# Two half-size last blocks, and the per-group sums written ahead of exp: a graph layer on one core

## The chip, the cores and the metric

The kernel runs on one core of a Trainium2 chip. The metric is device time in microseconds (us) of one execution. Nine runs of the kernel before gave a median of 2788.3 us, from 2753.89 to 2828.07.

## The reference, cut to what matters

One message-passing layer of a graph network, with a residual and a layer norm, in float32: 12,500 nodes and 200,000 edges of 64 features, the edges sorted by their target `dst`.

```python
gates = ssp(edge_attr @ We1 + be1) @ We2 + be2              # ssp(v) = softplus(v) - log 2
gates = gates * (1 - sigmoid(5.0 * (edge_weight - 3.5)))    # the cutoff
h = ssp(concat(x[src], x[dst]) @ Wn1 + bn1) @ Wn2 + bn2
message_sum = zeros.at[dst].add(h * gates)
new = x + (ssp(message_sum @ Ws1 + bs1) @ Ws2 + bs2)
out = layernorm(x + new)                                    # over the 64 features, eps 1e-5
```

## The kernel before, in words

**Groups.** The edges are worked on in 391 groups of 512, each as four tiles of 128. The rows `x[src]` are gathered, 14 groups ahead, by GpSimd's indirect DMA (L230), and some by single-row DMAs that the queues of SP and ScalarE issue (L256). The targets of a half group lie within 42 nodes, so the part of layer 1 that belongs to `dst` comes from a table row range (L285), and the scatter is a matmul with a one-hot matrix (L292) that DVE makes.

**One step.** A Python loop writes the instructions down by hand; each engine works through its own instructions in that order, and waits on semaphores of the others where data asks for it. With `i` as the step, TensorE does: transposes of group i+1 (L306, L303), the biases of layer 1 (L318, group i+1) and of layer 2 (L353, group i), `scatter(i-1)` (L382), `layer1_edge(i+1)` (L323), `layer1_node(i+1)` (L329) and `layer2(i)` (L360, L365). ScalarE does `xcopy` (L313, PSUM to SBUF, what L329 reads), `exps` (L340) and `logs` (L343) of group i+1, and issues nine row DMAs between them. DVE does `window(i-1)` (L399: two additions of the scattered sums, 64 x 42 each, into the SBUF tile `sums`), `hcut(i)` (L374), `message(i)` (L378, what the next scatter reads), `softplus(i+1)` (L348, what layer 2 of group i+1 reads) and `onehot(i+3)` (L292). The place in `sums` at which `window` adds is read from SBUF into registers of DVE's sequencer (L390).

**Buffers.** `z` is a PSUM tile of two banks, of which two exist. Layer 1 of group g writes three quarters of the tile: L323 a half of the first bank, L329 the other half and the first half of the second bank. `exps(g)` reads all three. The last quarter is lent: `scatter(g-2)` writes its sums into the free quarter of `zs[g]`, and `window(g-2)` reads them there. The framework orders the accesses to such a tile by the order in which the program writes them down, whatever the part of the tile: in this kernel `window(i-1)` is written behind `exps(i+1)`, and so the first addition waits for ScalarE's exp of group i+1 (the built program has that one wait on it). `exps(i+1)` itself waits for L329 and for an older softplus.

**Blocks.** The nodes are finished in blocks of 512 (a first one of 212, then 24 of 512): as soon as all edges of a block must have been added, `node_block` makes eleven parts of it (fetch of x, first layer L418, clamp, exp and log, centring, second layer L446 and L449, addition, square, variance, root, scaling, store), and `BLOCK_STEPS` spreads these over later steps. The last block waits for the last group and runs alone behind it.

Of the kernel before, what the change touches and what calls it, by code (L numbers as in the profile page):

```python
# [57 lines left out]
P = 128  # L58
# [12 lines left out]
BEHIND = 4  # L71


BLOCK_STEPS = ((2, 3, 4, 4, 6, 7, 8, 9, 10, 14), (2, 3, 3, 4, 5, 6, 7, 8, 9, 10), (1, 2, 1, 2, 3))
ROWS = (7, 9)
READ = 8
ROWS_FROM = -1
# [8 lines left out]
def node_blocks(N):  # L86

    first = N % NB
    assert N > NB and first % 2 == 0 and first <= HE
    sizes = ([first] if first else []) + [NB] * (N // NB)  # L90
    return [(sum(sizes[:i]), n) for i, n in enumerate(sizes)]


# [29 lines left out]
def gnn_resnorm_kernel(ctx: ExitStack, tc: tile.TileContext, a: dict, out: bass.AP, E: int):  # L123
# [277 lines left out]
    def node_block(first, n, pool):  # L401


        nq = -(-n // HE)
        p = min(P, n // 2)
        t = {}
        rows = slice(first, first + n)

        def tile3(name):
            return pool.tile([P, 2, 2, D], F32, name=name, bufs=3)[:p, :nq]  # L410

        def small(name):
            return pool.tile([P, 2, 2], F32, name=name, bufs=2)[:p, :nq]

        def hidden(z):
            t["z"] = z[:, :HE]
            for q in range(nq):
                nc.tensor.matmul(t["z"], ws1[:, q].rearrange("f o d -> f (o d)"),  # L418
                                 sums[:, first + q * HE : first + (q + 1) * HE], start=q == 0, stop=q == nq - 1,
                                 skip_group_check=True)  # L420

        def fetch():
            t["y"] = tile3("y")
            nc.sync.dma_start(t["y"], x[rows, :].rearrange("(q p k) d -> p q k d", q=nq, k=2))

        def center():
            mean = small("mean")
            nc.vector.tensor_reduce(mean, t["y"], AX.X, OP.add)
            nc.vector.scalar_tensor_tensor(t["y"], mean.to_broadcast([p, nq, 2, D]), -1.0 / D, t["y"], OP.mult, OP.add)

        def clamp():
            t["l"], t["zb"] = (pool.tile([P, HE], F32, name=name, bufs=2) for name in ("l_s", "zb"))
            nc.vector.tensor_scalar(t["l"], t["z"], packed["bs1"], BIG, OP.add, OP.min)
            nc.vector.tensor_scalar(t["zb"], t["z"], packed["bs1"], None, OP.add)

        def logs():
            nc.scalar.activation(t["l"], t["l"], AF.Exp)
            nc.scalar.activation(t["l"], t["l"], AF.Ln, bias=half, scale=0.5)

        def ssp():  # L440
            nc.vector.scalar_tensor_tensor(t["l"], t["zb"], -LN2, t["l"], OP.add, OP.max)

        def layer2(z):
            slots = t["l"].rearrange("f (p k) -> f k p", k=2)
            t["u"] = z[:p, :HE].rearrange("p (q k d) -> p q k d", q=2, k=2)
            nc.tensor.matmul(z[:p, :HE], ones3[:, :p], rs3.rearrange("q k d -> q (k d)"), start=True,  # L446
                             stop=False, skip_group_check=True)
            for k in range(2):
                nc.tensor.matmul(t["u"][:, :, k, :], slots[:, k, :p], ws2, start=False, stop=k == 1,  # L449
                                 skip_group_check=True)  # L450
# [12 lines left out]
        def root():  # L463
            t["r"] = small("rstd")
            nc.scalar.activation(t["r"], t["v"], AF.Ln, bias=eps[:p], scale=1.0 / D)
            nc.scalar.activation(t["r"], t["r"], AF.Exp, scale=-0.5)

        def scale():

            v, r = small("scaled"), t["r"]  # L470
            nc.vector.tensor_scalar(v, t["v"], 1.0 / D, EPS, OP.mult, OP.add)
            nc.vector.tensor_mul(v, v, r)
            nc.vector.scalar_tensor_tensor(v, v, -0.5, r, OP.mult, OP.mult)
            nc.vector.scalar_tensor_tensor(r, v, 1.5, r, OP.add, OP.mult)
            nc.vector.tensor_mul(t["y"], t["y"], r.to_broadcast([p, nq, 2, D]))

        def store():
            nc.sync.dma_start(out[rows, :].rearrange("(q p k) d -> p q k d", q=nq, k=2), t["y"])
# [10 lines left out]
    with tc.manual_schedule():  # L489
# [124 lines left out]
        with tc.tile_pool(name="finish", bufs=1) as finish:  # L614
# [12 lines left out]
            for i in range(-1, last - 1):  # L627
                now = parts.pop(i, [])
                early = [part for part in now if part.tensor]
                at(load, i + LOADS)  # L630
                read_rows(i, 0, ROWS[0])
                fetch(i, 0, ROWS[0])
                if i >= 0:
                    at(gather, i + AHEAD)
                transposes(i + 1, ("load", i + 1), ("gather", i + 1), ("onehot", i + 1))
                xcopy(i + 1)
                read_rows(i, 1, ROWS[1])
                fetch(i, 1, ROWS[1] - 6)
                layer1_bias(i + 1)
                at(layer2_bias, i)  # L640
                if i >= 1:
                    scatter(i - 1, zs[i + 1][:, 1, HE : HE + 2 * W])
                layer1_edge(i + 1)
                layer1_node(i + 1)
                exps(i + 1)
                fetch(i, 1, 3)
                logs(i + 1)
                fetch(i, 1, 3)
                at(window, i - 1)
                at(layer2, i)  # L650
                for part in early:
                    part.tensor(tx_tile())
                at(hcut, i)
                at(message, i)
                softplus(i + 1)
                for part in early:
                    part.others()
                at(onehot, i + 3)
                for part in now:
                    if not part.tensor:  # L660
                        part.others()
                complete = i
                if blocks and complete >= blocks[0][1] - PREPARE and not begun:
                    begun = node_block(*blocks[0][0], finish)
                    begun.pop(0).others()
                if blocks and complete >= blocks[0][1]:
# [6 lines left out]
            assert len(blocks) == 1 and begun and not parts  # L673


            begun.pop(2).others()
            transposes(last, ("load", last), ("gather", last), ("onehot", last))
            xcopy(last)
            layer1_bias(last)
            layer2_bias(last - 1)  # L680
            scatter(last - 2, zs[last][:, 1, HE : HE + 2 * W])
            layer1_edge(last)
            layer1_node(last)
            for some in (edge, node):
                exps(last, some)
                logs(last, some)
            square, variance, root, scale, store = (part.others for part in rest)
            square()
# [6 lines left out]
            layer2_edge(last)  # L695
            softplus(last, node)
# [4 lines left out]
            variance()  # L701
            root()
# [5 lines left out]
            hidden, clamp = begun.pop(0)  # L708
            hidden(gh_tile())
            scale()  # L710
            clamp()
            store()
            for part in begun:
                node_part(part)


# [150 lines left out]
```

## Time and profile before

| | |
|---|---|
| median of nine runs | 2788.3 us |
| the profiled execution | 2772.95 us, its span 2771.2 us |
| TensorE busy | 2201.4 us (79%), granted clock 0.824 of full |
| DVE, ScalarE, GpSimd busy | 1050.1, 968.3, 1431.7 us |
| from the last scatter's first matmul (2756.20 us) to the end | 15.0 us |
| `window`, both additions (L399) | 0.41 us |

The profile is one execution recorded by the hardware. A row of the timeline has start, duration, engine, line, operation, tiles and shapes, the number of instructions, and in brackets the idle time of the engine before it with what ended it. PE is TensorE, PEld its weight loads, ACT ScalarE, POOL GpSimd. A float32 matmul shows as two records. Ends of matmuls are modelled, so what waits for a matmul can start later than its row ends. The granted clock is recorded in pieces that are multiples of 3.41 us, at 1.0 or 0.5.

### The profile page before, as it was taken

How to read it: one execution, taken by the hardware profiler on the slowest of the kernel's cores; microseconds unless marked ns; L12 is line 12 of the kernel's file. 1: busy time of each engine (PE TensorE's matmuls, PEld its weight loads, DVE VectorE, ACT ScalarE, POOL GpSimd, SP SyncE). 2: the span in 40 equal slices, each digit the busy share in tenths (PEclk: the TensorE clock that was granted, in tenths of full speed). 3: DMA queues.
4: the chain of work that ended last, by engine and by line, in shares of the span. 5: the costliest groups of instructions: out<-in, count | busy, mean ns of one | idle time of the engine just before them, and what ended most of it. 6: DMA issues, size and time to landing. Idle time of an engine off the chain costs nothing.

```text
span 2771.2 us, 47838 instructions
## 1 busy us (share of the span) xinstructions
PE 2201.4 (79%) x11373; PEld 1765.4 (64%) x11373; DVE 1050.1 (38%) x2767; ACT 968.3 (35%) x1318; POOL 1431.7 (52%) x1520
## 2 busy tenths in 40 slices
PE   2478877788888887888877887888878788888788
PEld 1456666666666666666666666666666667666676
DVE  1333333333334333333333333434333433344345
ACT  0133333333333333333333333333333333333344
POOL 7245555545555555555555555555555545555530
PEclk9997788877888788778888879888888877777888
DMA  6222222212222222212222222222222222222220
GB/s 155 94 54 49 46 46 48 46 44 46 48 46 47 49 50 48 47 45 50 51 46 49 52 47 52 51 51 52 49 49 47 51 47 49 51 50 49 49 51 24
DMA packets 150911, 143.53 MB, mean 52 GB/s; under 512 B 51887, under 2 KB 98395, under 8 KB 150626
## 3 DMA queue, kind: packets, MB, share of 16 engines
q1 hardware_dynamic: 94090, 88.26, 11.3%
q0 software_dynamic: 48512, 49.77, 9.8%
q10 hardware_dynamic: 8024, 2.37, 0.4%
q8 instruction: 97, 1.59, 0.2%
q14 instruction: 188, 1.54, 0.2%
HBM read 130.59 MB, written 9.63 MB: 51 GB/s over the span
## 4 chain that ended last, share of the span: by engine, by line
PE 62%; issue 13%; another core or an unknown queue 9%; DVE 8%; ACT 4%; ACTq 3%; DVEq 1%; DMA 0%; SPq 0%
PE z L329 15%; PE gh L365 11%; PE z L382 11%; PE tx L306 7%; PE gh L360 7%; PE z L323 6%; ACT xT L313 3%; ACTq L256 3%; DVE h L374 3%; DVE msg L378 2%; PE gh L353 1%; PE z L318 1%; PE tx L418 1%; DVE sums L399 1%
## 5 line engine op out<-in xcount | busy, mean ns | idle before, releaser
L230 POOL DMA_INDIRECT xg<-in_x,src_i x1516 | 1431.5, 944 | 1246.1 <-PE z L382 418.7
L329 PE MATMUL z<-xT,wns 106*128 106x256 f32 x1564 | 572.5, 503 | 113.2 <-ACT xT L313 101.1
L340 ACT ACTIVATE u<-z 128x768 f32<-128x768 f32 x392 | 317.0, 809 | 920.4 <-issue 473.3
L382 PE MATMUL z<-xg,msg 128*128 128x84 f32 x1556 | 310.7, 330 | 347.1 <-DVE msg L378 247.8
L399 DVE TENSOR_TENSOR sums<-sums,z 64x42 f32 x778 | 152.9, 197 | 1121.1 <-issue 913.2
L382 PEld LDWEIGHTS z<-xg,msg 128*128 128x128 f32 x1556 | 243.1, 223 | 506.5 <-DVE msg L378 328.0
L329 PEld LDWEIGHTS z<-xT,wns 106*128 106x128 f32 x1564 | 374.6, 249 | 250.5 <-ACT xT L313 164.8
L365 PE MATMUL gh<-consts,s 128*128 128x64 f32 x3128 | 474.6, 305 | 0.0
L365 PEld LDWEIGHTS gh<-consts,s 128*128 128x128 f32 x3128 | 474.1, 231 | 0.0
L313 ACT COPY xT<-tx 106x512 f32<-106x512 f32 x391 | 228.5, 584 | 671.4 <-PE tx L306 248.6
L343 ACT ACTIVATE u<-u,one 128x768 f32<-128x768 f32 x392 | 365.9, 934 | 68.9 <-issue 56.8
L348 DVE SCALAR_TENSOR_TENSOR s<-u,z 128x768 f32<-128x768 f32 x392 | 369.0, 942 | 11.2 <-ACT u L343 10.1
L360 PEld LDWEIGHTS gh<-consts,s 128*128 128x128 f32 x1564 | 320.9, 253 | 45.4 <-DVE s L348 2.0
L374 DVE TENSOR_TENSOR h<-gh,cut 128x256 f32<-128x256 f32 x391 | 165.9, 424 | 449.5 <-PE tx L306 157.7
L323 PE MATMUL z<-eT,consts 128*128 128x256 f32 x782 | 312.0, 488 | 0.0
L360 PE MATMUL gh<-consts,s 128*128 128x128 f32 x1564 | 310.3, 334 | 1.7 <-DVE s L348 1.7
L306 PE MATMUL tx<-consts,xg 128*106 128x128 f32 x1517 | 260.1, 296 | 6.5 <-DMA wns<-table 6.5
L306 PEld LDWEIGHTS tx<-consts,xg 128*106 128x106 f32 x1517 | 202.1, 160 | 10.7 <-issue 8.0
L378 DVE TENSOR_TENSOR msg<-gh,h 128x256 f32<-128x256 f32 x391 | 165.8, 424 | 13.4
L353 PE MATMUL gh<-row,ones 3*128 3x512 bf16 x391 | 158.1, 404 | 0.0
L323 PEld LDWEIGHTS z<-eT,consts 128*128 128x128 f32 x782 | 147.9, 235 | 0.7 <-issue 0.7
L292 DVE TENSOR_TENSOR xg<-consts,rel 128x168 f32<-128x168 f32 x391 | 127.6, 327 | 0.0
(93 smaller groups left out, 604.0 us busy)
## 6 DMA issues: line engine op xcount, KB each, us to landing
xr<-in_x ACTq DMA_DIRECT2D x3328, 0.2 KB
eT<-in_eT SPq DMA_DIRECT2D x195, 256.0 KB
xr<-in_x SPq DMA_DIRECT2D x2688, 0.2 KB
xg<-in_x,src_i POOLq DMA_INDIRECT x1516
wns<-table SPq DMA_DIRECT2D x782, 21.0 KB
table<-tb SPq DMA_DIRECT2D x14, 448.0 KB
sums<-in_xT SPq DMA_DIRECT2D x7, 455.0 KB
y<-in_x SPq DMA_DIRECT2D x24, 128.0 KB
```

The lines of the kernel that those rows point to most:

```text
L230: note(("gather", g), nc.gpsimd.indirect_dma_start(out=xg[:, k, :D], out_offset=None, in_=x, in_offset=bass.IndirectOffsetOnAxis(ap=src_i[ ...
L306: ins = nc.tensor.transpose(tx[:, k, :], xgs[g][:, k, :DW], ident)
L313: note(("xcopy", g), nc.scalar.copy(xT, xTs[g]))
L323: nc.tensor.matmul(zs[g][:, 0, :HE], we1.rearrange("a h d -> a (h d)"), eTs[g], start=False, stop=True, skip_group_check=True)
L329: nc.tensor.matmul(zn, wns[:, g % REST, h, :], xTs[g][:, h], start=True, stop=True, skip_group_check=True)
L340: nc.scalar.activation(us[g][:, part], z_of(g)[:, part], AF.Exp)
L343: nc.scalar.activation(us[g][:, part], us[g][:, part], AF.Ln, bias=one)
L348: nc.vector.scalar_tensor_tensor(ss[g].rearrange("p i t e -> p (i t e)")[:, part], us[g][:, part], BIG, z_of(g)[:, part], OP.min, OP.max)
L360: nc.tensor.matmul(v[:, 0, t], ss[g][:, 0, t, :], we2, start=False, stop=False, skip_group_check=True)
L365: nc.tensor.matmul(ghs[g][:, 1, 2 * t + h, :], ss[g][:, 1 + h, t, :], wn2, start=False, stop=h == 1 and t == 1, skip_group_check=True)
L374: nc.vector.tensor_mul(hs[g], ghs[g][:, 1], cut[:, g, :].to_broadcast([P, K, D]))
L382: ins = nc.tensor.matmul(sc, msgs[g][:, 2 * t : 2 * t + 2, :].rearrange("p h f -> p (h f)"), xgs[g][:, 2 * t : 2 * t + 2, D:DW], start=t = ...
```

## The change

Three edits:

1. In the loop, `window(i-1)` is written behind `scatter(i-1)`, ahead of layer 1 and `exps` of group i+1; before, it stood behind `logs(i+1)` and its row DMAs. The same is done for the last groups, behind the loop.
2. The last 512 nodes are two blocks of 256. In such a block a tile has one node of 64 features for each of two halves in a partition (`kk = 1`) where others have two, so each instruction works on half as many columns.
3. The first of these two blocks is begun beside the last two groups; only the second waits for the last group. The block ahead of them keeps one more part (its square) in the steps.

```diff
-BLOCK_STEPS = (..., (1, 2, 1, 2, 3))
+BLOCK_STEPS = (..., (1, 2, 1, 2, 3, 4))
...
-    sizes = ([first] if first else []) + [NB] * (N // NB)
+    sizes = ([first] if first else []) + [NB] * (N // NB - 1) + [HE] * 2
...
+        kk, cols = 2, HE
+        if n == HE:
+            nq, kk, cols = 2, 1, P
...
-            return pool.tile([P, 2, 2, D], F32, name=name, bufs=3)[:p, :nq]
+            return pool.tile([P, 2, kk, D], F32, name=f"{name}{kk}", bufs=3 if kk == 2 else 2)[:p, :nq]
...
-            t["z"] = z[:, :HE]
+            t["z"] = z[:, :cols]
...
                 if i >= 1:
                     scatter(i - 1, zs[i + 1][:, 1, HE : HE + 2 * W])
+                at(window, i - 1)
                 layer1_edge(i + 1)
                 layer1_node(i + 1)
                 exps(i + 1)
                 fetch(i, 1, 3)
                 logs(i + 1)
                 fetch(i, 1, 3)
-                at(window, i - 1)
                 at(layer2, i)
...
+                if i == last - 2 * PREPARE:
+                    first_half, final = (node_block(*block, finish) for block, _ in blocks[-2:])
...
             scatter(last - 2, zs[last][:, 1, HE : HE + 2 * W])
+            window(last - 2)
+            scale()
+            store()
             layer1_edge(last)
             layer1_node(last)
...
-            window(last - 2)
+            z = z_tile()
+            hidden, clamp = first_half.pop(0)
+            hidden(z[:, 0, :])
+            clamp()
...
+            logs1.others()
+            scatter(last - 1, tx_tile()[:, : 2 * W])
             softplus(last, node)
             layer2_node(last)
-            hcut(last - 1)
-            message(last - 1)
-            scatter(last - 1, tx_tile()[:, : 2 * W])
...
+            window(last - 1)
+            ssp1.others()
+            hidden2(z[:, 1, :])
             hcut(last)
             message(last)
+            add1()
             scatter(last, tx_tile()[:, : 2 * W])
-            window(last - 1)
+            square1.others()
             window(last)
...
```

More of the change, by code (lines that the diff above doesn't have):

```diff
@@ L71 @@
 BEHIND = 4
-BLOCK_STEPS = ((2, 3, 4, 4, 6, 7, 8, 9, 10, 14), (2, 3, 3, 4, 5, 6, 7, 8, 9, 10), (1, 2, 1, 2, 3))
+BLOCK_STEPS = ((2, 3, 4, 4, 6, 7, 8, 9, 10, 14), (2, 3, 3, 4, 5, 6, 7, 8, 9, 10), (1, 2, 1, 2, 3, 4))
 ROWS = (7, 9)
@@ L409, in tile3 @@
         def tile3(name):
-            return pool.tile([P, 2, 2, D], F32, name=name, bufs=3)[:p, :nq]
+            return pool.tile([P, 2, kk, D], F32, name=f"{name}{kk}", bufs=3 if kk == 2 else 2)[:p, :nq]
         def small(name):
-            return pool.tile([P, 2, 2], F32, name=name, bufs=2)[:p, :nq]
+            return pool.tile([P, 2, kk], F32, name=f"{name}{kk}", bufs=2)[:p, :nq]
         def hidden(z):
-            t["z"] = z[:, :HE]
+            t["z"] = z[:, :cols]
             for q in range(nq):
                 nc.tensor.matmul(t["z"], ws1[:, q].rearrange("f o d -> f (o d)"),
-                                 sums[:, first + q * HE : first + (q + 1) * HE], start=q == 0, stop=q == nq - 1,
+                                 sums[:, first + q * cols : first + (q + 1) * cols], start=q == 0, stop=q == nq - 1,
                                  skip_group_check=True)
@@ L423, in fetch @@
             t["y"] = tile3("y")
-            nc.sync.dma_start(t["y"], x[rows, :].rearrange("(q p k) d -> p q k d", q=nq, k=2))
+            nc.sync.dma_start(t["y"], x[rows, :].rearrange("(q p k) d -> p q k d", q=nq, k=kk))
         def center():
@@ L428, in center @@
             nc.vector.tensor_reduce(mean, t["y"], AX.X, OP.add)
-            nc.vector.scalar_tensor_tensor(t["y"], mean.to_broadcast([p, nq, 2, D]), -1.0 / D, t["y"], OP.mult, OP.add)
+            nc.vector.scalar_tensor_tensor(t["y"], mean.to_broadcast([p, nq, kk, D]), -1.0 / D, t["y"], OP.mult, OP.add)
         def clamp():
-            t["l"], t["zb"] = (pool.tile([P, HE], F32, name=name, bufs=2) for name in ("l_s", "zb"))
+            t["l"], t["zb"] = (pool.tile([P, cols], F32, name=f"{name}{kk}", bufs=2) for name in ("l_s", "zb"))
             nc.vector.tensor_scalar(t["l"], t["z"], packed["bs1"], BIG, OP.add, OP.min)
@@ L443, in layer2 @@
         def layer2(z):
-            slots = t["l"].rearrange("f (p k) -> f k p", k=2)
-            t["u"] = z[:p, :HE].rearrange("p (q k d) -> p q k d", q=2, k=2)
-            nc.tensor.matmul(z[:p, :HE], ones3[:, :p], rs3.rearrange("q k d -> q (k d)"), start=True,
+            slots = t["l"].rearrange("f (p k) -> f k p", k=kk)
+            wide = 2 * kk * D
+            t["u"] = z[:p, :wide].rearrange("p (q k d) -> p q k d", q=2, k=kk)
+            nc.tensor.matmul(z[:p, :wide], ones3[:, :p], rs3.rearrange("q k d -> q (k d)")[:, :wide], start=True,
                              stop=False, skip_group_check=True)
-            for k in range(2):
-                nc.tensor.matmul(t["u"][:, :, k, :], slots[:, k, :p], ws2, start=False, stop=k == 1,
+            for k in range(kk):
+                nc.tensor.matmul(t["u"][:, :, k, :], slots[:, k, :p], ws2, start=False, stop=k == kk - 1,
                                  skip_group_check=True)
@@ L474, in scale @@
             nc.vector.scalar_tensor_tensor(r, v, 1.5, r, OP.add, OP.mult)
-            nc.vector.tensor_mul(t["y"], t["y"], r.to_broadcast([p, nq, 2, D]))
+            nc.vector.tensor_mul(t["y"], t["y"], r.to_broadcast([p, nq, kk, D]))
         def store():
-            nc.sync.dma_start(out[rows, :].rearrange("(q p k) d -> p q k d", q=nq, k=2), t["y"])
+            nc.sync.dma_start(out[rows, :].rearrange("(q p k) d -> p q k d", q=nq, k=kk), t["y"])
         return [Part(None, fetch), Part(hidden, clamp), Part(None, logs), Part(None, center), Part(None, ssp),
@@ L661, in gnn_resnorm_kernel @@
                         part.others()
+                if i == last - 2 * PREPARE:
+                    first_half, final = (node_block(*block, finish) for block, _ in blocks[-2:])
+                    first_half.pop(0).others()
+                    final.pop(0).others()
+                if i == last - PREPARE:
+                    first_half.pop(2).others()
+                    final.pop(2).others()
                 complete = i
-                if blocks and complete >= blocks[0][1] - PREPARE and not begun:
+                if len(blocks) > 2 and complete >= blocks[0][1] - PREPARE and not begun:
                     begun = node_block(*blocks[0][0], finish)
                     begun.pop(0).others()
-                if blocks and complete >= blocks[0][1]:
+                if len(blocks) > 2 and complete >= blocks[0][1]:
                     steps = next(steps for steps in BLOCK_STEPS if i + steps[-1] < last - 1)
@@ L672, in gnn_resnorm_kernel @@
                     begun = None
-            assert len(blocks) == 1 and begun and not parts
-            begun.pop(2).others()
+            assert len(blocks) == 2 and blocks[0][1] < last and not begun and not parts
+            variance, root, scale, store = (part.others for part in rest)
+            variance()
             transposes(last, ("load", last), ("gather", last), ("onehot", last))
             xcopy(last)
+            root()
             layer1_bias(last)
@@ L686, in gnn_resnorm_kernel @@
                 logs(last, some)
-            square, variance, root, scale, store = (part.others for part in rest)
-            square()
-            window(last - 2)
+            z = z_tile()
+            hidden, clamp = first_half.pop(0)
+            hidden(z[:, 0, :])
+            clamp()
             for g in range(last - 1, last + 1):
@@ L695, in gnn_resnorm_kernel @@
             layer2_edge(last)
+            hcut(last - 1)
+            message(last - 1)
+            logs1, ssp1, (hidden2, add1), square1, variance1, root1, scale1, store1 = first_half
+            logs1.others()
+            scatter(last - 1, tx_tile()[:, : 2 * W])
             softplus(last, node)
             layer2_node(last)
-            hcut(last - 1)
-            message(last - 1)
-            scatter(last - 1, tx_tile()[:, : 2 * W])
-            variance()
-            root()
+            window(last - 1)
+            ssp1.others()
+            hidden2(z[:, 1, :])
             hcut(last)
             message(last)
+            add1()
             scatter(last, tx_tile()[:, : 2 * W])
-            window(last - 1)
+            square1.others()
             window(last)
-            hidden, clamp = begun.pop(0)
+            hidden, clamp = final.pop(0)
             hidden(gh_tile())
-            scale()
+            variance1.others()
             clamp()
-            store()
-            for part in begun:
+            root1.others()
+            final.pop(0).others()
+            scale1.others()
+            store1.others()
+            for part in final:
                 node_part(part)
```

## The prediction

> **What bounds the kernel now.** I read the page first (busy shares, clock row, chain), then the timeline of one step near the end, where nothing disturbs the loop, then the groups behind L399, and last the step by step times of the whole loop.
>
> ```profile
> PE 2201.4 (79%) x11373; PEld 1765.4 (64%) x11373; DVE 1050.1 (38%) x2767; ACT 968.3 (35%) x1318; POOL 1431.7 (52%) x1520
> PEclk9997788877888788778888879888888877777888
> PE 62%; issue 13%; another core or an unknown queue 9%; DVE 8%; ACT 4%; ACTq 3%; DVEq 1%; DMA 0%; SPq 0%
> ```
>
> No engine is full; TensorE carries 62% of the chain (1718 of 2771 us), and its granted clock is under full from the third slice on. The loop is a ring, seen in the timeline of steps 383 and 384:
>
> ```profile
> 2723.49 0.42 DVE L378 TENSOR_TENSOR msg<-gh,h 128x256 f32<-128x256 f32 x1
> 2723.83 0.94 DVE L348 SCALAR_TENSOR_TENSOR s<-u,z 128x768 f32<-128x768 f32 x1
> 2723.97 0.68 PE L382 MATMUL z<-xg,msg 128*128 128x84 f32 x4
> ...
> 2724.48 0.63 PE L323 MATMUL z<-eT,consts 128*128 128x256 f32 x2
> 2724.69 0.33 DVE L292 TENSOR_TENSOR xg<-consts,rel 128x168 f32<-128x168 f32 x1
> ...
> 2724.95 1.03 PE L329 MATMUL z<-xT,wns 106*128 106x256 f32 x4
> ...
> 2726.02 0.81 ACT L340 ACTIVATE u<-z 128x768 f32<-128x768 f32 x1 [1.97 <-PE z L329]
> ...
> 2726.86 0.41 DVE L399 TENSOR_TENSOR sums<-sums,z 64x42 f32 x2 [1.51 <-ACT u L340]
> ...
> 2727.31 0.42 DVE L374 TENSOR_TENSOR h<-gh,cut 128x256 f32<-128x256 f32 x1
> ```
>
> The message (L378) ends at 2723.91; TensorE scatters it (2723.97), goes on without a pause to L323 (2724.48), L329 and layer 2, then DVE takes h (2727.31) and the next message, 4.27 us a step. TensorE pauses only while DVE does h and message (0.50 us before L382). DVE's softplus and one-hot run beside L382 and L323, and the additions (L399) wait for exp:
>
> ```profile
> L399 DVE TENSOR_TENSOR sums<-sums,z x778: 190/198/205, 153.5 to 2750.9; 64x42 f32 x195
> ...
>   issue: 913.2, 313
>   ACT u L340: 202.9, 79
> ```
>
> Over steps 20 to 369 a step takes 6.79 us, not 4.27: 0.98 from message to the scatter's end, 4.92 from there to h, 0.88 for h and message.
>
> **The change in the loop.** DVE's order does not change: additions, h, message, softplus, one-hot. What changes is who waits for whom. Written behind the scatter, the additions wait for L382 alone, no longer for exp. But they now stand ahead of L323, L329 and exp in the program, all of which use the z tile whose last quarter the additions read. In the built program of the changed kernel L323 waits for the second addition, and exp does; before, L323 waited for nothing of DVE. So the ring gets a new link: scatter, additions, L323. And the additions stand in DVE's queue behind softplus (0.94) and one-hot (0.33) of the step before, and behind whatever block part lies there. Behind the waiting L323, on TensorE, stand L329 and layer 2, and h, message and the next scatter wait for those.
>
> *Price of the new wait, one clean step.* From the rows above: one-hot ends at 2724.69 + 0.33 = 2725.02; additions 2725.05 to 2725.46; L323 some 0.07 later (one semaphore, as from L378's end to L382), at 2725.53, not 2724.48. That is 1.05 us of TensorE standing still; the step becomes 5.32 us.
>
> *Over the loop.* For steps 10 to 384 I took from the trace, for each step, the last of three things: scatter's semaphore, end of the DVE instruction ahead of the additions, end of their register load (L390, 0.53 us) plus 0.1; added 0.03 + 0.41 + 0.07, and compared the sum with the start of L323. L323 comes 1.37 us later in the mean (quarter points 0.94, 1.05, 1.85); in 150 steps the scatter is last, in 157 DVE, in 68 the register load. Part of that costs nothing, since L329 in many steps waited for the copied xT anyway: L329 comes 1.05 us later in the mean (quarter points 0.73, 1.01, 1.26). 389 steps x 1.05 = **+408 us**. Exp's own new wait adds nothing: it follows L329, which now comes later than the additions.
>
> *What goes.* In 56 of 365 steps h started within 0.07 us of the additions' end, on average 0.40 us after layer 2's modelled end: at most 56 x 0.40 = **-22 us**.
>
> *What may swallow some.* In 222 steps layer 2's semaphore came later than its modelled end, by 312 us in total; what delays it I can't name. If it is a point in time, the new wait vanishes in it; if it is a duration, nothing does. Bounds 0 and -312. I take a quarter, **-78 us**, nearer to none, because steps with a block's first layer (L418, 1.1 us of TensorE) were 0.9 us longer than the mean.
>
> *The clock.* Between 200 and 2650 us the trace has 441 pieces of 3.41 us at full clock and 276 at half. 146 of the full ones are followed by half. In those TensorE's rows cover 48% in the mean (22 to 65% for nine in ten), and the longest pause is 1.6 us at the median; in the 295 others 86%, and 0.39. So the clock falls after a piece with some 1.4 us or more of pauses. The new pause of 1.05 us stands 0.68 us from the old one of 0.50: a piece that holds both has 1.55 us of pauses, 55% covered. I take it that half, not a third, of the full pieces are then followed by half; with the rise as now (146 of 276) the share at half goes from 38 to 49%, the mean clock from 0.81 to 0.76. TensorE's 1718 us of the chain x (0.81/0.76 - 1) = **+113 us**. Bounds: 0 if no more pieces fall; if all steps run at half clock, a step is some 7.5 us (the slow steps of the trace: 1.2 + 5.4 + 0.88) plus 0.75 for the wait, 8.25, so (8.25 - 6.79) x 389 = +568 in place of all the terms here.
>
> The Trainium skill ("TensorE: Matmul & The Clock Gate", section "HAM oscillation — how this bites in real kernels") warns only of idle gaps over about 3.4 us. By that rule a pause of 1.05 us costs no clock, and the sum would be 113 us lower; this trace's clock fell after much shorter pauses, so the row decides.
>
> **The change at the end.** From 2756.2 us on, a block of 512 runs alone; half the columns save: L418 2.05 to about 1.0, L449 1.22 to 0.6, three ScalarE steps by 0.11 each (exp of 256 columns takes 0.38, of 768 0.81), five DVE steps by 0.13 each (0.42 at 256, 0.94 at 768): 2.6 us. The first half's work beside the last two groups puts two small matmul pairs (about 1.4 us at full clock) on TensorE between 2748 and 2757 and some 2 us on DVE, which is in the ring; if all of it is exposed +3.4, if none 0; I take 2. Net **-1 us**. Its scaling and store, and the fetches of both halves, lie beside other steps and are among what DVE's queue holds. This whole edit cannot be measured here.
>
> **Sum.** 2773 + 408 - 22 - 78 + 113 - 1 = 3193 us for a profiled execution like this one, which stood 15 us below the median of the nine: **3205 us**.
>
> **Rivals.**
> 1. *The late semaphores swallow the wait.* For: they come in three steps of five, and often exceed 1 us. Against: only 193 steps have over 0.3 us, and in the last 90 us, which have next to none, the wait is bare. 2773 + 408 - 22 - 312 = 2847 without a lower clock, 2960 with it: 2920 in the middle, with the 15 us.
> 2. *The clock stays at half.* For: even the undisturbed steps get 1.55 us of pauses, and a slow clock makes the ring longer. Against: at half clock TensorE's work fills the pieces again, and 146 of 276 slow pieces were followed by full ones. 2773 + 568 + 15: about 3360, up to 3500 if the late semaphores come on top.
> 3. *Not slower: h freed of the additions wins.* Place: the start of h, where 56 steps waited for the additions. Price: -22 us, and -3 at the end: 2763. It decides if the new wait is under 0.06 us a step, that is if DVE is free 0.4 us before the scatter ends. The one-hot ends before the scatter by that much in about one step of twenty; in the clean step it ends 0.37 us after it.
> 4. *Nothing happens in the loop*, because DVE's order is the same, and L323's wait is met before it counts: 2790. The clean step speaks against it as against the third.
>
> **Chances.** Forecast 0.64 (3040 to 3330), first rival 0.14, second 0.18, third 0.02, fourth 0.02. The range of 2930 to 3420 leaves out the last two, a third of the first and a third of the second. A change of under 1% could not be told from none here: faster by over 1% 0.01, within 1% 0.03, slower by over 1% 0.96.
>
> **What would show it.** In the profile after: L323 idles with the additions (L399) as releaser, some 300 to 500 us in total; the additions wait for L382 and no longer for L340; in the last 80 us, where the gathers are over, the step is 5.3 us or more instead of 4.27; the mean clock is about 0.76. The forecast is wrong if L323's idle time is there but the time from scatter to h is not longer (first rival), if the clock row reads 5 and 6 throughout (second), or if the additions end before the scatter's successor could start (third).

## The result and the profile after

The changed kernel took 3182.62 us (median of 20 runs, 3156.9 to 3204.74), the kernel before 2786.42 us (62 runs). The ratio is **1.1441 [1.1413, 1.1469]**: slower, and within 23 us of the 3205 us predicted. Medians count every run; the ratios, here and below, leave out the executions that stood clearly above the others of their kernel. Its profiled execution took 3193.88 us, with a span of 3192.0 us and a granted clock of 0.742 in place of 0.824.

From the page of the changed kernel: busy time of each engine, the clock row, the chain.

```profile
PE 2501.6 (78%) x11378; PEld 2011.7 (63%) x11378; DVE 1032.2 (32%) x2779; ACT 968.5 (30%) x1323; POOL 1432.1 (45%) x1520
PEclk9967677677677776778777676777776676777777
PE 61%; DVE 17%; issue 9%; another core or an unknown queue 7%; DVEq 4%; DMA 1%; POOL 1%; ACT 0%; ACTq 0%; SPq 0%; POOLq 0%
```

TensorE has five matmuls more than before, and 300 us more of busy time (2501.6 against 2201.4): the same work at a lower clock. The row that read 7 and 8 reads 6 and 7. DVE, 8% of the chain before, is 17% now.

The timeline of two steps near the end of the changed kernel (start, duration, engine, line, operation, tiles):

```profile
3130.59 0.42 DVE L378 TENSOR_TENSOR msg<-gh,h 128x256 f32<-128x256 f32 x1
3130.94 0.94 DVE L348 SCALAR_TENSOR_TENSOR s<-u,z 128x768 f32<-128x768 f32 x1
3131.07 0.68 PE L382 MATMUL z<-xg,msg 128*128 128x84 f32 x4
3131.80 0.33 DVE L292 TENSOR_TENSOR xg<-consts,rel 128x168 f32<-128x168 f32 x1
3132.04 0.41 DVE L465 TENSOR_REDUCE var<-y 128x4 f32<-128x256 f32 x1
3132.37 0.40 DVE L399 TENSOR_TENSOR sums<-sums,z 64x42 f32 x2
3132.82 0.70 PE L323 MATMUL z<-eT,consts 128*128 128x256 f32 x2 [1.07 <-DVE sums L399]
...
3138.48 0.41 DVE L399 TENSOR_TENSOR sums<-sums,z 64x42 f32 x2 [0.56 <-issue]
3138.94 1.22 PE L323 MATMUL z<-eT,consts 128*128 128x256 f32 x2 [1.62 <-DVE sums L399]
```

The new link is there as it was read from the program: softplus, one-hot, here also a block's reduction (L465), then the additions, and 0.05 us after those L323, with TensorE idle for 1.07 us. One step later the pause is 1.62 us and L323 takes 1.22 us in place of 0.70: the clock has gone to half. The 0.56 us ahead of the additions of that step are in part the load of their place in `sums` by DVE's sequencer (DVEq), 0.35 us on the chain of this execution:

```profile
3137.92 0.35 DVEq L390
```

All instances of the additions in the changed kernel: what ended their own wait, and who waited for them.

```profile
L399 DVE TENSOR_TENSOR sums<-sums,z x778: 130/197/205, 151.5 to 3171.3; 64x42 f32 x195
...
  PE z L382: 45.0, 71
  issue: 29.1, 65
...
  ACT u L340: 813.0, 196
  PEld z L323: 393.9, 359
  PE z L323: 331.6, 359
```

They wait for the scatter (L382) and never for exp (L340). Instead L323 waits for them in 359 recorded cases: 331.6 us of idle TensorE. All instances of L323 in the kernel before, which idled 0.7 us in all:

```profile
L323 PE MATMUL z<-eT,consts x782: 379/417/795, 141.1 to 2748.0; 128*128 128x256 f32 x196
...
  issue: 0.7, 2
```

For steps 20 to 369 I took the mean time of each part of a step from the rows of both traces, in us:

| | before | after | |
|---|---|---|---|
| step, from one h to the next | 6.79 | 7.83 | +1.04 |
| end of scatter to start of L323 | −0.18 | 0.99 | +1.17 |
| end of L323 to start of L329 (wait for xT) | 0.19 | −0.19 | −0.38 |
| L323, L329 and layer 2 themselves | 4.14 | 4.77 | +0.63 |
| modelled end of layer 2 to h | 0.95 | 0.57 | −0.38 |

### The profile page after: what moved, and what is told of

It reads as the page before. It is cut to its first block, busy times and chain, and to the rows that moved or that the text cites. A ratio compares the mean times of both kernels' runs of the same rounds, so it can differ in the third digit from the quotient of the medians.

```text
span 3192.0 us, 47723 instructions
## 1 busy us (share of the span) xinstructions
PE 2501.6 (78%) x11378; PEld 2011.7 (63%) x11378; DVE 1032.2 (32%) x2779; ACT 968.5 (30%) x1323; POOL 1432.1 (45%) x1520
## 4 chain that ended last, share of the span: by engine, by line
PE 61%; DVE 17%; issue 9%; another core or an unknown queue 7%; DVEq 4%; DMA 1%; POOL 1%; ACT 0%; ACTq 0%; SPq 0%; POOLq 0%
PE z L329 16%; PE gh L365 13%; PE z L323 11%; PE gh L360 8%; DVE h L374 4%; PE tx L306 4%; PE z L382 4%; DVE sums L399 4%; DVE s L348 3%; DVEq L390 3%; DVE xg L292 2%; DVE msg L378 1%; PE gh L353 1%; PE z L594 1%
## 5 line engine op out<-in xcount | busy, mean ns | idle before, releaser
L230 POOL DMA_INDIRECT xg<-in_x,src_i x1516 | 1431.9, 945 | 1630.9 <-PE z L382 522.6
L340 ACT ACTIVATE u<-z 128x768 f32<-128x768 f32 x392 | 317.0, 809 | 1587.8 <-issue 903.0
L323 PE MATMUL z<-eT,consts 128*128 128x256 f32 x782 | 395.7, 601 | 383.4 <-DVE sums L399 331.6
L329 PE MATMUL z<-xT,wns 106*128 106x256 f32 x1564 | 639.2, 553 | 1.0 <-ACT xT L313 1.0
L365 PEld LDWEIGHTS gh<-consts,s 128*128 128x128 f32 x3128 | 539.8, 259 | 0.1
L365 PE MATMUL gh<-consts,s 128*128 128x64 f32 x3128 | 531.9, 330 | 0.0
L329 PEld LDWEIGHTS z<-xT,wns 106*128 106x128 f32 x1564 | 449.3, 287 | 107.4 <-ACT xT L313 1.4
L382 PEld LDWEIGHTS z<-xg,msg 128*128 128x128 f32 x1556 | 241.0, 222 | 360.6 <-DVE msg L378 315.7
L382 PE MATMUL z<-xg,msg 128*128 128x84 f32 x1556 | 307.9, 328 | 200.9 <-DVE msg L378 173.6
L323 PEld LDWEIGHTS z<-eT,consts 128*128 128x128 f32 x782 | 160.5, 256 | 451.0 <-DVE sums L399 393.9
L360 PEld LDWEIGHTS gh<-consts,s 128*128 128x128 f32 x1564 | 371.1, 291 | 55.6 <-DVE s L348 0.7
L360 PE MATMUL gh<-consts,s 128*128 128x128 f32 x1564 | 359.2, 375 | 0.4 <-DVE s L348 0.4
L306 PE MATMUL tx<-consts,xg 128*106 128x128 f32 x1517 | 282.4, 314 | 6.5 <-DMA wns<-table 6.5
L306 PEld LDWEIGHTS tx<-consts,xg 128*106 128x106 f32 x1517 | 220.3, 172 | 10.7 <-issue 8.0
```

The costliest lines, as they stand in the source:

```text
L230: note(("gather", g), nc.gpsimd.indirect_dma_start(out=xg[:, k, :D], out_offset=None, in_=x, in_offset=bass.IndirectOffsetOnAxis(ap=src_i[ ...
L306: ins = nc.tensor.transpose(tx[:, k, :], xgs[g][:, k, :DW], ident)
L323: nc.tensor.matmul(zs[g][:, 0, :HE], we1.rearrange("a h d -> a (h d)"), eTs[g], start=False, stop=True, skip_group_check=True)
L329: nc.tensor.matmul(zn, wns[:, g % REST, h, :], xTs[g][:, h], start=True, stop=True, skip_group_check=True)
L340: nc.scalar.activation(us[g][:, part], z_of(g)[:, part], AF.Exp)
L360: nc.tensor.matmul(v[:, 0, t], ss[g][:, 0, t, :], we2, start=False, stop=False, skip_group_check=True)
```

## The experiments

The kernels ran on three further chips. Unexpectedly, the same kernel before took 1936.96 us on one (chip B), 2863.11 us on another (chip C), and 1936.19 us on a third (chip D). Every kernel is compared with the kernel before on its own chip. Times that were expected for a kernel before of 2786 us are compared by their ratio to it.

**The parts, one by one (chip B).** The theory: all of the loss is L323's wait on the additions, with the clock that it pulls down. The rival: part of it comes from the half-size blocks, or from exp's new wait.

Only the halves, with the additions back in their old place:

```diff
 # the changed kernel
-                at(window, i - 1)
                 layer1_edge(i + 1)
...
+                at(window, i - 1)
                 at(layer2, i)
```

> The changed kernel with the additions of the loop back behind the logs: what is left of the change are the two blocks of 256 and the last groups' new order. Theory (all of the loss is the wait of L323 on the additions in the loop): 2786 us within 1% of the kernel before, clock 0.82, step 6.8 us; the last three groups have the new order and may cost some us. Rival (the half blocks and their work beside the last groups cost a part of the 396 us): 2830 us or more.

Measured: 1936.23 us, ratio 1.0002 [0.9992, 1.0011]. The halves and the rearranged end cost nothing that can be measured, and gain nothing.

Only the move, on the kernel before:

```diff
 # the kernel before
+                at(window, i - 1)
                 layer1_edge(i + 1)
...
-                at(window, i - 1)
                 at(layer2, i)
```

> The kernel before with nothing but the additions of the loop written behind the scatter, as in the changed kernel. Theory: as slow as the changed kernel, 3150 to 3210 us, ratio 1.13 to 1.155, clock 0.74 to 0.76. Rival (the half blocks matter): clearly under 3100 us.

Measured: 2640.01 us, ratio 1.3651 [1.3603, 1.3698], far above the 1.13 to 1.155 expected. Since the halves alone cost nothing on this chip, the whole loss on it is the move. The clock row from the page of the halves alone:

```profile
PEclk9999999999999999999999999999999999999998
```

and from the page of the move alone:

```profile
PEclk9977888988898887888897977887868877878886
```

The timeline of two steps of the move alone:

```profile
1208.47 0.68 PE L382 MATMUL z<-xg,msg 128*128 128x84 f32 x4
1209.19 0.33 DVE L292 TENSOR_TENSOR xg<-consts,rel 128x168 f32<-128x168 f32 x1
1209.44 0.16 DVE L471 TENSOR_SCALAR scaled<-var 128x4 f32<-128x4 f32 x1
...
1210.24 0.43 DVE L475 TENSOR_TENSOR y<-y,rstd 128x256 f32<-128x256 f32 x1
1210.98 0.41 DVE L399 TENSOR_TENSOR sums<-sums,z 64x42 f32 x2 [0.32 <-issue]
1211.45 0.70 PE L323 MATMUL z<-eT,consts 128*128 128x256 f32 x2 [2.30 <-DVE sums L399]
1211.98 1.79 PE L329 MATMUL z<-xT,wns 106*128 106x256 f32 x4
...
1218.35 0.70 PE L323 MATMUL z<-eT,consts 128*128 128x256 f32 x2 [0.74 <-DVE sums L399]
1218.88 1.03 PE L329 MATMUL z<-xT,wns 106*128 106x256 f32 x4
```

In a bare step (the second) the pause is 0.74 us. In the first the five instructions of a block's scaling (L471 to L475) stand in DVE's queue ahead of the additions; TensorE idles 2.30 us, and L329 then takes 1.79 us instead of 1.03. The two steps show the chain of causes: what is queued on DVE sets the pause, and the clock falls with the longer pause. That the pause lowers the clock is tested further down.

The same move, a little less far, twice: behind L323, so that L329 waits in its place, and behind L329, so that only exp waits.

```diff
 # the kernel before; the second puts it behind layer1_node(i + 1)
                 layer1_edge(i + 1)
+                at(window, i - 1)
                 layer1_node(i + 1)
...
-                at(window, i - 1)
                 at(layer2, i)
```

> As the move alone, but the additions are written one line later, behind L323 and ahead of L329. In the built program the additions then wait for L323 and L329 waits for the additions; exp waits for them as in the changed kernel. Theory (what costs is how long TensorE stands behind the additions, each 0.03 + 0.41 + 0.07 us plus what DVE has to finish first): in a clean step TensorE stands 0.6 us instead of 1.05, and more of the wait for xT is covered; 2900 to 3030 us, clock about 0.78. Rival (exp's new wait on the additions costs, wherever they stand ahead of it): as slow as the move alone, 3150 us or more.

Measured: 2524.11 us, ratio 1.2927 [1.2822, 1.3033]. The loss is smaller than the move's, as expected, but far above the 1.04 to 1.09 that the expected times make. From the groups of its profiled execution, which took 2574.36 us (busy, mean ns, idle time ahead with what ended it):

```profile
L329 PE MATMUL z<-xT,wns 106*128 106x256 f32 x1564 | 534.5, 473 | 307.8 <-DVE sums L399 306.0 <-ACT xT L313 1.2 <-issue 0.6
```

> As the move alone, but the additions are written behind L329 and ahead of exp: the additions wait for L329, exp waits for the additions, and TensorE waits for neither. Theory: exp starts some 0.5 us later, the next step has room for it (softplus and the copy of xT are needed more than 0.5 us later in a clean step), and h is no longer held by the additions: 2755 to 2830 us. Rival (exp's wait is what makes the changed kernel slow): 2950 us or more.

Measured: 1937.53 us, ratio 1.0015 [0.9999, 1.0031]. All instances of the additions in that kernel:

```profile
  PE z L329: 280.3, 341
...
  ACT u L340: 754.5, 377
```

Here the additions wait for L329 and exp is recorded as waiting for the additions, and on this chip it costs nothing that can be measured, as expected; ScalarE, busy for 50% of the span, seems to have the time. So the loss comes on whichever instruction of TensorE is made to wait, and is gone as soon as no such instruction stands behind the additions.

**The one-hot and the clock (chip C, beside the changed kernel itself).**

> The changed kernel again, beside the next three. Theory: the move alone is the change, so it measures as the run of the move alone did if it is the same chip (2640 us where the kernel before takes 1937), or near 3180 us where the kernel before takes 2786. Rival (the half blocks gain or lose beside the move): over 15 us away from that.

Measured: 3225.54 us, ratio 1.1261 [1.1209, 1.1313], clock 0.742.

Is the queue on DVE the size of the wait? The one-hot goes behind the additions, into the next step:

```diff
 # the changed kernel
                 at(window, i - 1)
+                at(onehot, i + 2)
...
-                at(onehot, i + 3)
```

> The changed kernel with the one-hot of group i+2 written behind the additions of the next step, not ahead of them, so that DVE has 0.33 us less to do before the additions. Theory (DVE's queue ahead of the additions sets the pause at full clock, the scatter at half): the pause from the scatter's end to L323 falls by about 0.3 us where DVE was last, TensorE's pauses in a clean step go from 1.55 to 1.2 us and the clock falls less often; 2100 to 2400 us where the kernel before takes 1937, 2980 to 3120 where it takes 2786. Rival (the scatter's semaphore and the additions themselves set it): unchanged within 2%.

Measured: 3138.74 us, ratio 1.0959 [1.0903, 1.1015], within what was expected, and 87 us less than the changed kernel beside it. From the scatter to L323 it takes 0.79 us instead of 1.00: 0.21 us a step, 81 us over 389 steps. One instruction of 0.33 us accounts for a fifth of the wait.

Does the clock rise if the pause is filled? Two more bias matmuls of layer 2 (three rows, bf16) stand between the scatter and L323; the last leaves the bias as it was.

```diff
 # the changed kernel
+                at(bias_again, i)      # two matmuls as L353
                 at(window, i - 1)
                 layer1_edge(i + 1)
```

> The changed kernel with two more matmuls on TensorE in each step, between the scatter and L323: they compute the bias of layer 2 of group i twice again into the same place, so that nothing depends on them anew and the result stays. They fill some 0.4 us of TensorE's pause at full clock, 0.9 at half. Theory of two prices (the pause itself, and the clock that falls because of it): the wait stays, the clock rises; where the kernel before takes 1937 us the clock goes from 0.84 to 0.95 or more and the time from 2640 to 2150 to 2350 us; where it takes 2786 us, from 3180 to 2950 to 3100. Rival (the pause alone is the price, the clock falls for other reasons): unchanged, or up to 100 us slower for the added work.

Measured: 3247.54 us, ratio 1.1311 [1.1254, 1.1369], clock 0.735: not higher, and 22 us more than the changed kernel beside it. The theory missed here, and the rival's range holds; either the clock was not a price, or these matmuls don't act on it.

Where else could the additions go? Behind the message:

```diff
 # the changed kernel
-                at(window, i - 1)
                 layer1_edge(i + 1)
...
                 at(message, i)
+                at(window, i - 1)
```

> The changed kernel with the additions of the loop behind the message, ahead of softplus, so that h is never held by them and neither L323 nor exp has a new wait: they wait for exp as before. Theory: the kernel before's time, less what the additions held h: 0 to 1% faster than the kernel before, at its clock. Rival (softplus, now 0.41 us later, or the later release of the z tile holds layer 2): slower than the kernel before by over 1%.

Measured: 2843.08 us, ratio **0.9904 [0.9868, 0.994]**, within what was expected. This version is about 1% faster than the kernel before (0.7% by the medians of all runs), a small gain, under the 2% from which a change is called faster here. TensorE all but never waits on the additions (L323 idles 1.7 us for them in all). The 20 us gained are about the 22 us that the working gave at most for h held by the additions; that this is their cause is not shown, since no trace of the kernel before was taken on this chip.

**The clock again (chip D).** The pause of the changed kernel filled with two float32 matmuls of 128 rows, and one bias matmul that restores the bias:

```diff
 # the changed kernel
+                at(fill_pause, i, 2)   # 2 x (128x128 by 128x128, float32), then L353 again
                 at(window, i - 1)
                 layer1_edge(i + 1)
```

> The changed kernel with the pause between the scatter and L323 filled by other matmuls than in the pause-filling run before: two of 128 rows in float32 (constants by constants, written where layer 2 of group i will be, then the bias of layer 2 is written over them again). In that run pieces of 3.41 us that TensorE's rows covered whole stayed at half clock (152 pieces, median cover 1.00 with the fill, 0.79 without): the fill of three rows seems not to count. Theory (a full piece of work of all rows lifts the clock, and the clock is a price of its own): the clock rises by 0.06 or more against the changed kernel; where the kernel before takes 2786 to 2863 us the ratio to it falls from 1.13 or 1.14 to 1.04 to 1.10, where it takes 1937 us from 1.365 to 1.10 to 1.25. Rival (the clock is set by something that TensorE's work doesn't change, or the fill's own 0.65 to 1.3 us eats the gain): ratio unchanged or higher.

Measured: 2381.26 us, ratio 1.2274 [1.2251, 1.2296], within what was expected. Its profiled execution took 2414.62 us at a clock of 0.941. The clock row of its page:

```profile
PEclk9999999899989899999899999999898998899896
```

More work, and less time: chip B had given 1.3651 for the move without filling. The wait is still there (1.05 us from the scatter to L323 against 0.98), but L323, L329 and layer 2 take 3.42 us a step in place of 4.05. So the clock is a price of its own, beside the wait, if the two chips are alike; the run with three stages below has both in one execution.

The same filling in the version with the additions behind the message, ahead of layer 2's bias:

```diff
 # the kernel with window behind message
         gh = gh_tile()
+        fill(gh, 2)                     # 2 x (128x128 by 128x128, float32)
```

> The changed kernel with the additions behind the message (0.990 of the kernel before) and two matmuls of 128 rows on constants ahead of the bias of layer 2, in the pause in which TensorE waits for the message (0.50 us in a clean step). Theory (fewer pauses, a higher clock): where the kernel before takes 2786 to 2863 us a ratio of 0.93 to 0.98, clock 0.84 or more; where it takes 1937 us, 1.00 to 1.02, since its clock is full. Rival (the late semaphores make pauses of 1 to 3 us that 0.43 us cannot fill, and the fill costs time at half clock): 1.00 to 1.06.

Measured: 2030.95 us, ratio 1.0487 [1.0469, 1.0504], a larger loss than expected. The clock was 0.996, but at 0.98 on this chip there was nothing left to win, and the filling itself lay on the path (TensorE 97% of the chain). The version without the filling was not run on this chip, so how much of the 4.9% is the filling's is not shown.

The two fillings had run on different chips. One kernel has all three cases, by step: none up to 129, the bias matmuls from 130, the float32 ones from 260 on.

```diff
 # the changed kernel
+                if i >= 130:
+                    at(fill_pause, i)   # 2 x L353; from step 260: 2 x float32, then L353
                 at(window, i - 1)
```

> The changed kernel, with additional matmuls in the pause between scatter and L323 that change with the step: none up to step 129, two bias matmuls of 3 rows (bf16) from step 130 to 259, two float32 matmuls of 128 rows and one bias matmul from step 260 on. The first filling was tried alone on a chip like that of the result, where the clock did not rise (0.735 against 0.742), the second alone on a quicker chip, where it did (0.941 against 0.838); here both are on one chip in one execution, so the chip cannot be the difference. Theory, the kind of matmul decides: the 3-row matmuls count little for the clock. Then on a quick chip the first two stages take about 6.5 us a step at a mean clock near 0.84 and the third about 5.9 near 0.95; on a chip with late semaphores the first two 7.8 to 8.0 near 0.73 and the third 7.0 to 7.5 at 0.8 or more. Rival, the chip decides: the second and the third stage are alike within 0.1 us a step, both quick (5.9) on a quick chip or both at 7.8 to 8.0 on the other kind.

Measured: 2563.02 us (one run), with the profile's windows of the three stages (busy us and number for PE, PEld, DVE, ACT, POOL; granted clock; share and rate of the DMA):

```profile
219.00:876.00 657.00, 550.55 (x3043) 440.35 (x3041) 255.09 (x686) 254.36 (x334) 394.09 (x418) 0.88 0.22 52
907.00:1737.00 830.00, 764.87 (x3839) 569.01 (x3840) 316.64 (x861) 305.11 (x417) 462.47 (x490) 0.82 0.21 50
1766.00:2420.00 654.00, 603.69 (x3661) 476.44 (x3660) 288.46 (x792) 268.00 (x378) 396.76 (x421) 0.95 0.24 56
```

The clock is 0.88 without filling, 0.82 with the bias matmuls and 0.95 with the float32 ones, in one execution, although TensorE's rows cover 92% of both filled stages (764.87 of 830 us, 603.69 of 654). A step takes 6.10, 6.59 and 6.05 us, with 0.89, 1.01 and 1.16 us from the scatter to L323.

The stages also differ in their place in the loop, and that counts. In the move alone (chip B, no filling) the same three stretches of steps take 6.13, 6.50 and 6.79 us, with a wait of 0.88, 0.98 and 1.08 us, at clocks of 0.87, 0.835 and 0.815. Beside these the bias matmuls change little, and the float32 ones bring the clock of the last stretch from 0.815 to 0.95 and take 0.7 us off its step. And in the kernel with float32 filling throughout, on the same chip D, the middle stretch has a clock of 0.96, against 0.82 here with the bias matmuls. So the kind of the matmul decides, not the chip and not the place in the loop. The first stage was quicker than expected (6.5), since it comes early in the loop, and the third slower (5.9), since its wait is longer; the difference between the two fillings is the one expected.

**The late semaphores (chip D).** Are the gathers what makes TensorE's semaphores late? From group 14 on, the kernel before without gathers: its output lacks the right `x[src]` for those groups.

```diff
 # the kernel before, in the function of the gathers
+        if g >= AHEAD:
+            xgs[g] = xgs[g - AHEAD]
+            return
```

> The kernel before without GpSimd's gathers from group 14 on (left out: the rows x[src] of these groups; the rows of the group 14 before are used again). One question: are the late semaphores of layer 2 (312 us in 222 steps where the kernel takes 2773 us; none in the last 90 us, where no gathers run; none in the fast runs of 1937 us) made by the gathers? If so, the step falls from 6.8 to 5 us or less and layer 2's end is followed by h within 0.1 us; where the kernel before takes 1937 us, at most 5% less. If not, 2600 us or more where the kernel before takes 2786.

Measured: 1904.17 us (one run) against 1936.19. It fell on a chip that has no late semaphores (modelled end of layer 2 to h: 0.12 us), so it says nothing about them.

## Why the prediction was right, point by point

- **The new link and its place**: right. L323 waits for the additions, the additions for L382 alone; on chip B the halves alone cost nothing and the move alone costs all. Exp's own new wait costs nothing there, as the place behind L329 shows.
- **Size of the wait**: 408 us predicted. Measured are 1.17 us a step at L323, less 0.38 that L329 had waited for xT anyway: 0.79 × 389 = 308 us. The start of L329 alone moves by 1.00 us, near the 1.05 of the working, but 0.21 of that is L323 at a lower clock. Near the end the steps that ran at full clock take 5.25 to 5.7 us, with 5.32 predicted; the others there take 6.3 to 11.8 us.
- **The clock**: 113 us predicted, the term most mis-sized. L323, L329 and layer 2 take 0.63 us a step longer: 0.63 × 389 = 245 us. Between 200 and 2650 us, 55% of the pieces at full clock are followed by half (half was assumed). But the rise was taken "as now", at 53% of the half pieces, and it was 46%; the mean clock there is 0.73, not 0.76. The step that failed is this one, and the ground for it given beside the second rival, "at half clock TensorE's work fills the pieces again". In the changed kernel, from 200 to 3050 us, 200 of 210 pieces ahead of a rise are covered by TensorE's rows for at least 97%, and of 244 that stayed at half 186 are covered less: the new pause is long enough to spoil a piece even at half clock. With 0.73 the working's own formula gives 1718 × (0.81/0.73 − 1) = 188 us; the other 57 us it does not give, and what they are was not tested. Nor is "some 1.4 us or more of pauses" a bound: in the changed kernel falls come after pieces covered for up to 77%, that is after 0.8 us of pauses.
- **h freed of the additions and the late semaphores**: −100 us predicted together, −0.38 × 389 = −149 us measured. Before, 222 steps had a late semaphore, for 312 us; after, 188 steps, for 193 us. So the late semaphores swallowed 119 us, not 78, two fifths of what the first rival had; the remaining 30 us are near the 22 taken for h.
- **Sum**: the three terms miss by −100, +132 and −49 us. Their sum is right to 17 us because they cancel, which is luck; the 1 us between 3193 and 3193.88 is chance. (3193 and 15 are 3208; the 3205 on record is 3 us less than its own sum.)
- **The other rivals**: the clock does not stay at half; h freed does not outweigh the wait; and the wait counts.

The Trainium skill ("TensorE: Matmul & The Clock Gate", section "HAM oscillation — how this bites in real kernels") counts only gaps of over about 3.4 us. These runs go against it: in the move alone 131 pieces at full clock are followed by half, with a longest pause of 0.75 us at the median and of 2.63 us at most. The same page's section "A second HAM failure mode: psum-queue depth-cycling" tells of a kernel in which frequent short idles make the clock swing; that agrees with these rows.

What stays open: what makes TensorE's semaphores late on two of the four chips. On chips B and D h follows the modelled end of layer 2 by 0.04 us in most steps; on the chip of the result and on chip C it does not. The traces do show with what it goes. In the kernel before on the chip of the result (steps 20 to 384), h follows 1.06 us later in the mean where layer 2's modelled end falls into a run of GpSimd's gathers (L230; 299 steps), and 0.28 us elsewhere (66 steps); in the changed kernel it is 1.25 us (98 steps) and 0.29 (267). So the lateness goes with the gathers there, and the longer step meets them less often, which fits the 119 us. On chip B the same gathers delay nothing (0.04 us in 191 such steps of the move alone), so they can't be the whole cause. Why L323 needs to wait at all was not tried either: it writes the first bank of the tile and the additions read the second, but the framework orders the tile as a whole.

## What to carry to other kernels

When an instruction is moved ahead of others in the program, look in the built program at every later access to the same tile: each can become a waiter, and what counts is which engine it stands on. A wait on the engine that carries the ring costs the whole queue of the engine it waits for, block work and register loads included; a wait on an engine with time to spare cost nothing here, and neither did work put behind the last instruction of the ring (behind the message, about 1% faster). The pause on TensorE was paid twice here, once as itself and once as a lower clock, and the second was four fifths of the first (245 us to 308).

## What the runs showed of the hardware

- **The same kernel took 1937 us on two chips and 2786 to 2863 us on two others.** On the latter the semaphores of TensorE come long after the modelled end of its matmuls, already in the set-up. Two rows of the kernel before on the chip of the result:

```profile
39.53 3.36 PE L590 MATMUL z<-consts,sums 65*128 65x128 f32 x14 [4.29 <-issue]
...
76.80 0.58 ACT L592 COPY tb<-z 128x512 f32<-128x512 f32 x1 [37.91 <-remote]
```

  The matmuls end at 42.9 us by the model, and the copy that reads them starts at 76.80, right after TensorE's semaphore, the only one that it waits for, is recorded as raised (76.78). In the move alone, on chip B, such a copy follows every 3 us:

```profile
36.95 0.58 ACT L592 COPY tb<-z 128x512 f32<-128x512 f32 x1 [3.55 <-PE z L590]
...
39.93 0.58 ACT L592 COPY tb<-z 128x512 f32<-128x512 f32 x1 [2.40 <-PE z L590]
```

- **The price of a change depends on the chip**: the move cost 36.5% on chip B, where the kernel before ran at a clock of 0.98, and the change 14.4% and 12.6% on the two chips where the clock was about 0.8 already. In the rows of the table above, the move adds 1.15, −0.03, 0.87 and −0.07 us a step on chip B (the move alone against the halves alone), and 1.17, −0.38, 0.63 and −0.38 on the chip of the result: there part of the new wait fell into waits that were there before, and the clock had less to lose.
- **The clock falls easily and rises almost only after a fully covered piece** of 3.41 us: in four traces (before, after, the move alone, the float32 filling), 508 of 521 pieces ahead of a rise are covered for at least 97%, and none ahead of a fall is covered for more than 78%. A covered piece is not enough: 146 of 222 such pieces at half clock were followed by a rise before, 200 of 258 after.
- **Matmuls of three rows in bf16 do not keep it up, those of 128 rows in float32 do**: 0.82 against 0.95 in one execution. The difference is in the falls: with the bias matmuls 45 of 156 pieces at full clock are followed by half, those 45 covered for 90% at the median; with the float32 ones 13 of 173. Rows and type changed together, so which of the two decides stays open.
